# Two quads of matrices to a block in the product stage, with one pool of eight PSUM banks

## The chip, the cores and the metric

The kernel runs on one core of one Trainium2 chip. The metric is the device time of one execution in microseconds (us). Five engines each run their own instructions in order: TensorE (PE in the profile; its weight loads are listed as PEld), VectorE (DVE), ScalarE (ACT), GpSimd (POOL) and SyncE (SP), which here issues most transfers (DMAs). They wait for each other on semaphores. [...]

## The reference

The reference is a network of two layers on 16 images of 128 channels and 32 x 32 pixels. The first layer has an attention, then a part that convolves the 1024 tokens of an image with 16 long filters and mixes the channels with a matrix for each filter. The second layer has two 3 x 3 convolutions and a mixture of experts. The change lies in the long convolution, which the reference computes with Fourier transforms:

```python
Vf = jnp.fft.rfft(phi, n=n, axis=0)
Uf_p = jnp.fft.rfft(u, n=n, axis=1)
Uf_m = jnp.fft.rfft(u * sgn3, n=n, axis=1)
U_plus = jnp.fft.irfft(Vf[None, :, :, None] * Uf_p[:, :, None, :], n=n, axis=1)[:, :sl]
U_minus = jnp.fft.irfft(Vf[None, :, :, None] * Uf_m[:, :, None, :], n=n, axis=1)[:, :sl]
...
out = jnp.einsum('btkd,k,kde->bte', U_plus, s, Mpp)
out = out + jnp.einsum('btkd,k,kde->bte', U_minus, s, Mpm)
```

For one frequency the filters and the channel matrices fold into one complex matrix of 128 x 128, and what is left is its product with the 16 spectra of the images.

## The kernel before, in words

The kernel has three parts in time: the first layer up to the spectra, with the folding of the filters (0 to 395 us of the profiled execution), the product stage (395 to 684 us), and the inverse transform with the second layer (from 684 us).

The product stage handles the frequencies in 16 chunks (NCH). For each chunk c there are:

- The spectra v. `begin(c)` loads them from device memory (vd) in four transfers of four images each into `xc` (L764, SP), adds and subtracts their halves (L767, two instructions a transfer, POOL) and writes a negated copy (L768, one a transfer, POOL). v has two buffers, each xc one.
- The matrices g. `generate(c, q)`, for eight quads q, multiplies the folded filters `mst` with `ph` (L776, TensorE). Each product uses 32 rows of TensorE, so four of them (index r) stand beside each other, each with its own PSUM bank `pg`; a quad has 16 products. TensorE splits each float32 product into two, so the trace shows 32 records for a quad. Then the four banks are copied to SBUF: r = 1 by VectorE (L783), r = 3 by VectorE except in every fourth quad, the others by ScalarE (L785). g has two buffers, one for even chunks and one for odd.
- The product. `multiply(c, m, x, py, fresh)` multiplies g with v (L796, TensorE), for four values of m and two halves x. Each product uses 32 columns of TensorE; again 16 products, 32 records. Both halves of an m go to one bank `py`.
- The combination. The first half of py is copied to SBUF as `yt` (L822, ScalarE), and VectorE writes the sum and the difference of the second half, read from PSUM, and yt into `ys` (L824, L825). After the four m of a chunk four more additions follow (L832 to L835, POOL, in the last chunk VectorE), and ys is stored to device memory (yd) in two transfers (L839, SP). The next stage loads yd again (L945).

In the text, the loop (L808 to L842) puts one quad of chunk c+1 ahead of one half of chunk c, so that TensorE changes between them sixteen times a chunk, and `begin(c + 1)` comes first in a chunk. Six PSUM banks serve the quads (`psg`), two the sums (`psy`). In this stage the order of the instructions on each engine is left to the framework's scheduler, which starts from the text; in the two stages beside it, `tc.manual_schedule(engines=PINNED)` keeps the order of the text on PE, DVE, ACT and POOL. SP is not in PINNED. A tile of a pool waits until one of the pool's buffers is released by everything that read it.

Of the kernel before, what the change touches and what calls it, by code (L numbers as in the profile page):

```python
# [8 lines left out]
F32 = mybir.dt.float32  # L9
AF = mybir.ActivationFunctionType  # L10
ALU = mybir.AluOpType
AX = mybir.AxisListType
PSUM = bass.MemoryType.PSUM

P = 128
B, C, H, W = 16, 128, 32, 32
# [15 lines left out]
NM = NQ // 2  # L32
NCH = 16
JL = 8
CW = 2 * 2 * NM * JL
# [5 lines left out]
RG = P // KR  # L41
# [4 lines left out]
PINNED = {  # L46
    mybir.EngineType.PE, mybir.EngineType.DVE, mybir.EngineType.Activation, mybir.EngineType.Pool,
}
# [18 lines left out]
def metaformer_kernel(ctx: ExitStack, tc: tile.TileContext, io: dict, out: bass.AP):  # L67
    nc = tc.nc
# [26 lines left out]
    for n, (g_, b_, m_, v_) in enumerate(((V_G1, V_B1, V_M1, V_V1), (V_G2, V_B2, V_M2, V_V2))):  # L95
# [15 lines left out]
                name=nc.get_next_instruction_name(), ins=[], outs=[], act_func_set_id=EXP_LN  # L111
# [52 lines left out]
    with ExitStack() as l0:  # L164
# [581 lines left out]
        with ExitStack() as g0:  # L746
            gpl = [g0.enter_context(tc.tile_pool(name=f"gpl{i}", bufs=1)) for i in range(2)]
            cpl = g0.enter_context(tc.tile_pool(name="cpl", bufs=2))
            xcl = g0.enter_context(tc.tile_pool(name="xcl", bufs=1))
            psg = g0.enter_context(tc.tile_pool(name="psg", bufs=6, space=PSUM))  # L750
            psy = g0.enter_context(tc.tile_pool(name="psy", bufs=2, space=PSUM))
            gs, vs = {}, {}
            NB = EPR // 4

            def begin(c):

                gs[c] = gpl[c % 2].tile([P, CW, C], F32, name="g", tag="g")
                v = cpl.tile([P, 2 * NM * JL, 3, B], F32, name="v", tag="v")
                vs[c] = v
                vv = v.rearrange("p (x w) k b -> p x k b w", x=2)  # L760
                for i in range(B // BP):
                    bs = slice(i * BP, (i + 1) * BP)
                    xc = xcl.tile([P, BP, 2, 2, NM * JL], F32, name="xc", tag=f"xc{i}")
                    nc.sync.dma_start(xc.rearrange("p b x r w -> p b (x r w)"), vd[c, :, bs, :])  # L764
                    e, o = (xc[:, :, x].rearrange("p b r w -> p r b w") for x in range(2))
                    for x, op in enumerate((ALU.add, ALU.subtract)):
                        nc.gpsimd.tensor_tensor(vv[:, x, 1:, bs], e, o, op)  # L767
                    nc.gpsimd.tensor_scalar(v[:, :, 0, bs], v[:, :, 2, bs], -1.0, None, ALU.mult)  # L768

            def generate(c, q):  # L770

                pg = [psg.tile([P, 4, CW], F32, name="pg", tag="pg") for r in range(RG)]
                for i in range(4):
                    for r in range(RG):
                        rs = slice(r * KR, (r + 1) * KR)
                        nc.tensor.matmul(  # L776
                            pg[r][:, i], mst[rs, 4 * q + i, :], ph[rs, c, :], start=True, stop=True,
                        )
                for r in range(RG):
                    dst = gs[c].rearrange("p w (g q i) -> p g q w i", g=RG, q=NB)[:, r, q]  # L780
                    src = pg[r].rearrange("p i w -> p w i")
                    if r % 2 and (r == 1 or q % 4):
                        nc.vector.tensor_copy(dst, src)  # L783
                    else:
                        nc.scalar.copy(dst, src)  # L785

            def multiply(c, m, x, py, fresh):

                g, v = gs[c], vs[c]
                for kl in range(JL // RG):  # L790
                    for ri in range(2):
                        for grp in range(RG):
                            jl = RG * kl + grp
                            rows = slice(grp * 2 * B, (grp + 1) * 2 * B)

                            nc.tensor.matmul(  # L796
                                py[rows, x, kl, :],
                                v[:, (x * NM + m) * JL + jl, 1 - ri : 3 - ri, :]
                                .rearrange("p k b -> p (k b)"),
                                g[:, ((x * 2 + ri) * NM + m) * JL + jl, :],  # L800
                                start=(grp not in fresh), stop=(ri == 1), skip_group_check=True,
                            )
                            fresh.add(grp)

            begin(0)
            for q in range(NB):
                generate(0, q)
            for c in range(NCH):  # L808
                if c + 1 < NCH:
                    begin(c + 1)  # L810

                ys = cpl.tile([P, JL // RG, 2, NM, C], F32, name="ys", tag="ys")
                for m in range(NM):
                    py = psy.tile([P, 2, JL // RG, C], F32, name="py", tag="py")
                    fresh = set()
                    for x in range(2):
                        if c + 1 < NCH:
                            generate(c + 1, 2 * m + x)
                        multiply(c, m, x, py, fresh)
                        if x == 0:  # L820
                            t = cpl.tile([P, JL // RG, C], F32, name="yt", tag="yt")
                            nc.scalar.copy(t, py[:, 0])  # L822

                    nc.vector.tensor_tensor(ys[:, :, 0, m], py[:, 1], t, ALU.add)  # L824
                    nc.vector.scalar_tensor_tensor(  # L825
                        ys[:, :, 1, m], py[:, 1], -1.0, t, ALU.mult, ALU.add
                    )

                eng = nc.gpsimd if c + 1 < NCH else nc.vector
                e = cpl.tile([P, JL // RG, 2, C], F32, name="ye", tag="ye", bufs=1)  # L830
                yv = ys[:, :, 0]
                eng.tensor_tensor(e, yv[:, :, :2], yv[:, :, 2:], ALU.add)  # L832
                eng.tensor_tensor(yv[:, :, 2:], yv[:, :, :2], yv[:, :, 2:], ALU.subtract)
                eng.tensor_tensor(yv[:, :, 0], e[:, :, 0], e[:, :, 1], ALU.add)
                eng.tensor_tensor(yv[:, :, 1], e[:, :, 0], e[:, :, 1], ALU.subtract)  # L835
                for kl in range(JL // RG):
                    last = c + 2 >= NCH
                    j0 = kl * RG + (c - NCH + 2 if last else c) * JL
                    nc.sync.dma_start(  # L839
                        yd[last][j0 : j0 + RG].rearrange("g r b x e -> (g r b) (x e)"),  # L840
                        ys[:, kl].rearrange("p x m e -> p (x m e)"),
                    )  # L842


    gpool = ctx.enter_context(tc.tile_pool(name="gpool", bufs=1))
# [9 lines left out]
    with ExitStack() as c1:  # L855
# [557 lines left out]
        def collect(g, og):  # L1413

            pt = ps.tile([P, EG, CG], F32, name="pot", tag="s", bufs=1)
            nc.tensor.transpose(pt.rearrange("p i b -> p (i b)"), og, ident)
            nc.vector.tensor_copy(
                ot[:, :, g * EG : (g + 1) * EG].rearrange("p b i -> p i b"), pt[:, :, :B]
            )
# [34 lines left out]
        with tc.manual_schedule(engines=PINNED):  # L1454
            for pr in (7, *range(NPAIR - 1)):
                py = [ps.tile([P, N], F32, name=f"pfy{j}", tag="pfy") for j in range(2)]
# [7 lines left out]
                for j in range(2):  # L1464
                    b = 2 * pr + j
                    if j and pr % 2:
                        t = first.tile([P, N], F32, name="yt", tag="v", bufs=2)
# [133 lines left out]
```

## Time and profile before

| | |
|---|---|
| time, median of three runs | 1324.6 us (1319.44 to 1328.2) |
| span of the profiled execution, first to last instruction | 1322.2 us |
| product stage in it: first quad to last addition | 395.8 to 684.3 us |
| chunk in the middle of the stage | 16.91 us |
| TensorE busy in the span | 1216.7 us (92%) |
| L776, the quads | 155.3 us busy, 4096 records |
| L796, the products | 140.1 us busy, 4096 records |
| L785, copies of g by ScalarE | 153.1 us, 288 of 591 ns |
| L783, copies of g by VectorE | 145.8 us, 224 of 687 ns |
| L767, sums for v by POOL | 91.6 us, 128 of 741 ns |

The profiled execution's time is known as its span; what lies around the span is not listed. A line of the trace in order of time gives the start, the duration in us, the engine, the line of the kernel, the operation, the tile written and those read, the shapes and the number of instructions merged, and in brackets how long the engine was idle before and what ended that. "issue" means that it waited for nothing that the profile shows. Records of matmuls overlap, since a product starts while those before it are still on their way.

### The profile page before, as it was taken

How to read it: one execution, taken by the hardware profiler on the slowest of the kernel's cores; microseconds unless marked ns; L12 is line 12 of the kernel's file. 1: busy time of each engine (PE TensorE's matmuls, PEld its weight loads, DVE VectorE, ACT ScalarE, POOL GpSimd, SP SyncE). 2: the span in 40 equal slices, each digit the busy share in tenths (PEclk: the TensorE clock that was granted, in tenths of full speed). 3: DMA queues.
4: the chain of work that ended last, by engine and by line, in shares of the span. 5: the costliest groups of instructions: out<-in, count | busy, mean ns of one | idle time of the engine just before them, and what ended most of it. 6: DMA issues, size and time to landing. Idle time of an engine off the chain costs nothing. (4 is left out here: it accounts for less than half of the span.)

```text
span 1322.2 us, 33734 instructions
## 1 busy us (share of the span) xinstructions
PE 1216.7 (92%) x14116; PEld 990.8 (75%) x14116; DVE 907.2 (69%) x1982; ACT 705.2 (53%) x1424; POOL 503.3 (38%) x816
## 2 busy tenths in 40 slices
PE   4889999999998999999956999999999999996886
PEld 3777777777767888888846987989888888883443
DVE  5688887877765666776637767777778676772224
ACT  3777777777545666666623435545555454544111
POOL 2324545454685777777743111222212121110002
PEclk8899999999998999999987999999999999997998
DMA  7014343433344333333367211313122113007986
GB/s 268 17 35 140 118 134 112 144 124 121 114 149 145 127 125 127 127 121 119 107 235 182 70 48 49 88 27 111 32 80 64 33 49 127 17 24 260 374 329 255
DMA packets 87401, 162.99 MB, mean 123 GB/s; under 512 B 5584, under 2 KB 40784, under 8 KB 86864
## 3 DMA queue, kind: packets, MB, share of 16 engines
q1 hardware_dynamic: 86608, 158.33, 36.2%
q8 instruction: 111, 1.82, 0.6%
q0 software_dynamic: 640, 2.49, 0.5%
q14 instruction: 42, 0.34, 0.1%
HBM read 104.18 MB, written 56.62 MB: 122 GB/s over the span
## 5 line engine op out<-in xcount | busy, mean ns | idle before, releaser
L926 PE MATMUL pcv<-v,cw 128*128 128x256 f32 x1536 | 342.9, 380 | 0.0
L926 PEld LDWEIGHTS pcv<-v,cw 128*128 128x128 f32 x1536 | 286.8, 190 | 42.2 <-issue 5.7
L785 ACT COPY g<-pg 128x512 f32<-128x512 f32 x288 | 153.1, 591 | 102.8 <-PE pg L776 102.8
L783 DVE COPY g<-pg 128x512 f32<-128x512 f32 x224 | 145.8, 687 | 90.1 <-PE pg L776 90.1
L776 PE MATMUL pg<-ph,mst 32*128 32x128 f32 x4096 | 155.3, 287 | 4.5 <-ACT g L785 3.0
L776 PEld LDWEIGHTS pg<-ph,mst 32*128 32x128 f32 x4096 | 130.7, 190 | 30.8 <-issue 25.9
L796 PE MATMUL py<-g,v 128*32 128x128 f32 x4096 | 140.1, 276 | 3.8 <-POOL v L768 1.2
L796 PEld LDWEIGHTS py<-g,v 128*32 128x32 f32 x4096 | 105.3, 110 | 20.7 <-issue 2.4
L767 POOL TENSOR_TENSOR v<-xc 128x256 f32<-128x256 f32 x128 | 91.6, 741 | 71.6 <-PE py L796 62.5
L141 ACT ACTIVATE tok<-tok,sts 128x128 f32<-128x128 f32 x256 | 101.8, 481 | 23.8 <-POOL sts L1001 20.4
L132 DVE BATCH_NORM_STATS2 bst<-big 128x6 f32<-128x256 f32 x256 | 91.1, 417 | 19.5 <-PE big L154 12.1
L1066 POOL TENSOR_SCALAR sts<-bst 128x8 f32<-128x8 f32 x16 | 6.5, 406 | 235.7 <-DVE bst L132 235.7
L920 DVE TENSOR_TENSOR v<-pads 128x544 f32<-128x544 f32 x128 | 85.0, 723 | 9.9 <-ACT pads L1119 9.5
L618 PE MATMUL big<-u,mu 128*128 128x128 f32 (+4 forms) x384 | 86.0, 380 | 0.0
L274 POOL TENSOR_TENSOR xf<-ab 128x256 f32<-128x256 f32 x34 | 24.8, 730 | 132.0 <-DVE ab L241 131.9
L618 PEld LDWEIGHTS big<-u,mu 128*128 128x128 f32 x384 | 56.7, 191 | 18.0 <-issue 15.4
L1097 ACT ACTIVATE ct<-pcv,bn 128x256 f32<-128x256 f32 x64 | 30.3, 474 | 68.8 <-PE pcv L926 67.9
L551 PE MATMUL big<-wf,ub 128*128 128x256 f32 x256 | 62.0, 385 | 0.2
L149 PEld LDWEIGHTS big<-ident,x 128*128 128x128 f32 x384 | 47.3, 148 | 19.2 <-issue 7.2
L149 PE MATMUL big<-ident,x 128*128 128x128 f32 x384 | 53.6, 286 | 8.5 <-DVE x L1048 3.4
L1115 DVE TENSOR_TENSOR r<-pcv,cs 128x256 f32<-128x256 f32 x64 | 26.9, 420 | 49.0 <-PE pcv L926 48.2
L141 ACT ACTIVATE tt<-tt,sts 128x128 f32<-128x128 f32 x128 | 51.1, 480 | 9.2 <-POOL sts L1001 8.9
(231 smaller groups left out, 2271.3 us busy)
## 6 DMA issues: line engine op xcount, KB each, us to landing
we<-in_weight SPq DMA_DIRECT2D x32, 1024.0 KB, 9.7
vd<-xf SPq DMA_DIRECT2D x16, 1024.0 KB, 5.1
xc<-vd SPq DMA_DIRECT2D x64, 256.0 KB, 3.5
yd<-ys SPq DMA_DIRECT2D x32, 512.0 KB, 3.8
y<-yd SPq DMA_DIRECT2D x15, 896.0 KB, 6.5
x<-in_x SPq DMA_DIRECT2D x16, 512.0 KB, 4.1
mi<-in_M_phi SPq DMA_DIRECT2D x16, 512.0 KB, 4.9
xd<-x SPq DMA_DIRECT2D x16, 512.0 KB, 6.0
```

The costliest lines, as they stand in the source:

```text
L132: nc.vector.bn_stats(bst[:, j : j + 2, :].rearrange("p j s -> p (j s)"), src[:, j : j + 2, :].rearrange("p j c -> p c j"),)
L141: nc.scalar.activation(dst[:, j, :], src[:, j, :], AF.Identity, bias=nm[:, j : j + 1], scale=r[:, j : j + 1],)
L149: nc.tensor.transpose(pt[:, j, :], src[:, j * P : (j + 1) * P], ident)
L551: nc.tensor.matmul(dst, self.ub[:, q, :], wf[:, q, :], start=True, stop=True)
L618: nc.tensor.matmul(self.pa[:, a:hi], mu[:, NF - 1 - si, tap, :], self.u[:, a - tap : hi - tap], start=(tap == 0), stop=(tap == KU - 1),)
L767: nc.gpsimd.tensor_tensor(vv[:, x, 1:, bs], e, o, op)
L776: nc.tensor.matmul(pg[r][:, i], mst[rs, 4 * q + i, :], ph[rs, c, :], start=True, stop=True,)
L783: nc.vector.tensor_copy(dst, src)
L785: nc.scalar.copy(dst, src)
L796: nc.tensor.matmul(py[rows, x, kl, :], v[:, (x * NM + m) * JL + jl, 1 - ri : 3 - ri, :] .rearrange("p k b -> p (k b)"), g[:, ((x * 2 + ri) ...
L920: nc.vector.tensor_tensor(v[:, k], d[i], d[j], op)
L926: nc.tensor.matmul(pc[:, i], wt[:, dy, k, :], v[:, k, hf * HR + dy : hf * HR + dy + HR], start=(dy == 0), stop=(dy == 2),)
```

## The change

A block of the loop now has two quads of chunk c+1 and then both halves of one m of chunk c, so there are four blocks a chunk. `generate` is split: it only makes the products, and `collect` copies them out. A block's order in the text is: both quads, the copies of the first, the combination of the block before (`combine`, and after the last m of a chunk `finish`), then, in the first block of a chunk, `begin(c + 1)`, the copies of the second quad, both halves, and one ScalarE copy of all of py to `t`. The combination therefore reads both operands from t in SBUF. t has one buffer of twice the size. All PSUM tiles of the stage come from one pool of eight banks under one tag. The whole stage stands under `manual_schedule`. The number of products, of copies of g and of operations on POOL is as before.

```diff
-            psg = g0.enter_context(tc.tile_pool(name="psg", bufs=6, space=PSUM))
-            psy = g0.enter_context(tc.tile_pool(name="psy", bufs=2, space=PSUM))
+            psg = g0.enter_context(tc.tile_pool(name="psg", bufs=8, space=PSUM))
...
             def begin(c):
 
-                gs[c] = gpl[c % 2].tile([P, CW, C], F32, name="g", tag="g")
...
-                pg = [psg.tile([P, 4, CW], F32, name="pg", tag="pg") for r in range(RG)]
+                pg = [psg.tile([P, 4, CW], F32, name="pg", tag="p") for r in range(RG)]
...
+                return pg
+
+            def collect(c, q, pg):
+
                 for r in range(RG):
...
-            begin(0)
-            for q in range(NB):
-                generate(0, q)
-            for c in range(NCH):
-                if c + 1 < NCH:
-                    begin(c + 1)
-
-                ys = cpl.tile([P, JL // RG, 2, NM, C], F32, name="ys", tag="ys")
-                for m in range(NM):
-                    py = psy.tile([P, 2, JL // RG, C], F32, name="py", tag="py")
-                    fresh = set()
-                    for x in range(2):
-                        if c + 1 < NCH:
-                            generate(c + 1, 2 * m + x)
-                        multiply(c, m, x, py, fresh)
-                        if x == 0:
-                            t = cpl.tile([P, JL // RG, C], F32, name="yt", tag="yt")
-                            nc.scalar.copy(t, py[:, 0])
-
-                    nc.vector.tensor_tensor(ys[:, :, 0, m], py[:, 1], t, ALU.add)
-                    nc.vector.scalar_tensor_tensor(
-                        ys[:, :, 1, m], py[:, 1], -1.0, t, ALU.mult, ALU.add
-                    )
+            def finish(c, ys):
 
                 eng = nc.gpsimd if c + 1 < NCH else nc.vector
...
+            def combine(c, m, ys, t):
+
+                nc.vector.tensor_tensor(ys[:, :, 0, m], t[:, 1], t[:, 0], ALU.add)
+                nc.vector.scalar_tensor_tensor(
+                    ys[:, :, 1, m], t[:, 1], -1.0, t[:, 0], ALU.mult, ALU.add
+                )
+                if m == NM - 1:
+                    finish(c, ys)
+
+            with tc.manual_schedule(engines=PINNED):
+                begin(0)
+                gs[0] = gpl[0].tile([P, CW, C], F32, name="g", tag="g")
+                for q in range(NB):
+                    collect(0, q, generate(0, q))
+                waiting = None
+                for c in range(NCH):
+                    if c + 1 < NCH:
+                        gs[c + 1] = gpl[(c + 1) % 2].tile([P, CW, C], F32, name="g", tag="g")
+
+                    ys = cpl.tile([P, JL // RG, 2, NM, C], F32, name="ys", tag="ys")
+                    for m in range(NM):
+                        if c + 1 < NCH:
+                            pg = [generate(c + 1, 2 * m + x) for x in range(2)]
+                            collect(c + 1, 2 * m, pg[0])
+                        if waiting:
+                            combine(*waiting)
+                        if c + 1 < NCH:
+                            if m == 0:
+                                begin(c + 1)
+                            collect(c + 1, 2 * m + 1, pg[1])
+                        py = psg.tile([P, 2, JL // RG, C], F32, name="py", tag="p")
+                        fresh = set()
+                        for x in range(2):
+                            multiply(c, m, x, py, fresh)
+                        t = cpl.tile([P, 2, JL // RG, C], F32, name="yt", tag="yt", bufs=1)
+                        nc.scalar.copy(t, py)
+                        waiting = c, m, ys, t
+                combine(*waiting)
```

## The prediction

> **What bounds the kernel now.** I read the page's first part, then the windows of the product stage (395 to 684 us), then its order of time, and last the start of the next stage, which shows two engines that meet there as they will meet in the changed stage.
>
> ```profile
> PE 1216.7 (92%) x14116; PEld 990.8 (75%) x14116; DVE 907.2 (69%) x1982; ACT 705.2 (53%) x1424; POOL 503.3 (38%) x816
> 503.00:521.00 18.00, 18.00 (x555) 15.22 (x548) 12.55 (x24) 11.70 (x24) 13.82 (x18) 1.00 0.40 131
> ```
>
> In 18 us of the stage (columns PE, PEld, DVE, ACT, POOL, clock) TensorE is busy throughout at full clock, the others 65 to 77%. So the order on TensorE sets the time, and only what TensorE spends or waits counts.
>
> ```profile
> 504.18 0.98 PEld L776 LDWEIGHTS pg<-ph,mst 32*128 32x128 f32 x32 [0.20 <-issue]
> 504.50 0.41 DVE L824 TENSOR_TENSOR ys<-py,yt 128x256 f32<-128x256 f32 x1
> 504.83 0.41 DVE L825 SCALAR_TENSOR_TENSOR ys<-py,yt 128x256 f32<-128x256 f32 x1
> 505.28 0.81 PEld L796 LDWEIGHTS py<-g,v 128*32 128x32 f32 x32
> 505.37 1.07 ACT L785 COPY g<-pg 128x512 f32<-128x512 f32 x2 [1.04 <-PE pg L776]
> 505.41 1.29 DVE L783 COPY g<-pg 128x512 f32<-128x512 f32 x2 [0.17 <-PE pg L776]
> 506.29 0.98 PEld L776 LDWEIGHTS pg<-ph,mst 32*128 32x128 f32 x32 [0.20 <-issue]
> ...
> 674.52 1.77 PEld L796 LDWEIGHTS py<-g,v 128*32 128x32 f32 x64 [0.71 <-PE py L796]
> ```
>
> A quad is generated in 1.10 us (504.18 to 505.28), a half multiplied in 1.01: 2.11 together, 16.91 for a chunk of eight pairs. The 0.20 us ahead of each quad is put to "issue": TensorE waits for nobody, it changes from products 128x32 to 32x128. The single records show eight rounds of four in each train. Rounds follow at 0.112 (generate) and 0.109 us (multiply), but there is 0.218 to the first multiply round and 0.135 after it, 0.221 to the first generate round and 0.215 after it. Above the plain steps that is 0.107 + 0.026 + 0.111 + 0.103 = 0.347 us per pair of changes. The x64 row is two multiply trains without a gap; the stage's first load row, x36, runs from one quad into the next likewise.
>
> ```profile
> 694.94 0.43 DVE L965 TENSOR_TENSOR zt<-y 128x256 f32<-128x256 f32 x1 [10.63 <-DMA y<-yd]
> 694.96 0.99 POOL L958 TENSOR_TENSOR z<-y 128x256 f32<-128x256 f32 x1 [16.38 <-DMA y<-yd]
> 695.29 0.95 DVE L966 TENSOR_TENSOR zt<-y 128x256 f32<-128x256 f32 x1
> 695.91 0.90 POOL L959 TENSOR_TENSOR z<-y 128x256 f32<-128x256 f32 x1
> 696.16 0.94 DVE L967 TENSOR_TENSOR zt<-y 128x256 f32<-128x256 f32 x1
> 697.02 0.41 DVE L968 TENSOR_TENSOR zt<-y 128x256 f32<-128x256 f32 x1
> ```
>
> Here VectorE's operands both lie in SBUF while POOL reads SBUF. An operation of 0.41 us takes 0.95, POOL's of 0.73 takes 0.90 to 0.99, by turns. L824 and L825 above, with one operand in PSUM, take 0.41 although POOL is at work beside them.
>
> **The change, part by part.** T is the start of a block's first quad, T' of the next block's.
>
> *TensorE.* A block is now two quads and two halves with one pair of changes where there were two: 2 x 2.114 - 0.347 = 3.88 us. There are 15 chunks of 4 blocks with quads: 60 x 0.347 = 20.8 us less. The first block gains some 0.6 more: POOL's v still ends at 414.9, but both quads of that block then lie ahead of it, in time that TensorE now spends waiting (414.95 is the first multiply after a wait of 1.4).
>
> *The last chunk* has no quads. Now it takes from 670.2 to 682.2, because each half waits for a copy (L822) or an addition. Then it is 64 rounds x 0.109 = 7.0, the last product's end 0.27, copy 0.59, two additions 0.74, steps between 0.3: 8.9. I take 2.9 less; at worst nothing, since POOL's v for this chunk is due 2 us earlier than elsewhere. Gross gain 20.8 + 0.6 + 2.9 = 24.3.
>
> *Banks.* Eight banks hold both quads, and the sum py takes the first that is copied out: T + 1.19 + 0.59 = 1.8, needed at T + 2.0. The next block's first quad needs three others and one of the second quad, copied by about T + 3.3. Its second quad, due at T' + 1.0, needs all that are left: py and those of the second quad. py: its last product ends near T', the copy starts 0.18 after T' (as L822 does now) and is out at T' + 0.8, which fits by 0.2.
>
> *ACT.* The copy grows from 0.39 to 0.59 us and comes once a block where there were two: 5 x 0.59 + 0.59 = 3.5 at most of 3.88. It costs nothing while it ends before T' + 1.0. Its target t has one buffer where there were two, so it also waits for the additions on the t before: they end by T + 3.7 + r, in the worst case 0.3 after the copy could start, less than the stall on VectorE that r then makes anyway.
>
> *VectorE.* The two additions now stand between the copies of both quads; behind them wait the second quad's copies, and behind these the next second quad on TensorE. Additions alone: 0.33 + 0.33 us from start to start. In a block with odd m (two copies a quad, 0.60 apart): 1.24 + 2 x 0.60 + 0.67 + 0.60 + 0.69 = T + 4.40 = T' + 0.52; it fits. But the operand that was in PSUM is now t in SBUF, and POOL works through most of a chunk: 1.24 + 1.23 + 0.70 + 0.69 (L832 to L835) and 4 x (0.70 + 0.70 + 0.82) (L767, L768) = 12.7. From the rows at 694.94: the first addition waits for what is left (r) of POOL's operation, which keeps VectorE out for 0.60; then they alternate at 0.60 + 0.26 = 0.86. So the pair takes r + 0.86 + 0.33 in place of 0.67, and the last copy is out at T' + 1.04 + r: with 0.05 to TensorE a stall of 0.09 + r. r is between 0 and 0.60; I take the middle, 0.30, as nothing fixes the phase: 0.39 a stall. In even blocks ACT takes one of the copies, 0.60 less, and there is no stall; in the first block of a chunk POOL stands idle, since it waits for these very additions. So two stalls a chunk, 29 in all: 11.3 us back (2.6 to 20).
>
> [...]
>
> *POOL and SP.* The end of chunk c-1 (four operations, two yd stores) now stands ahead of the beginning of chunk c+1 (12 operations, four xc loads), and waits for the additions: from T0 + 2.6 (T0: start of the chunk), where POOL now starts v at T0 + 0.1. 2.6 + 12.7 + 1.6 held by VectorE (6 x 0.26) = T0 + 16.9; v is needed at T0 + 16.3 + 2.0. Covered by 1.4; if that cover goes, each us beyond costs 14 us. SP is not in the pinned set: xc is loaded as soon as POOL has freed its buffer, a chunk ahead, before the yd of the chunk after. I cost the move of six DMA issues at nothing for that reason. Moving the allocation of g issues nothing.
>
> **Sum.** 24.3 - 11.3 = 13.0. The profiled span of 1322.2 becomes 1309.2; the median shown, 1324.6, is 2.4 above that span (start and end outside it, and scatter), so 1311.6. With the bounds of r: 1303 to 1320.
>
> **Rivals.**
> 1. The additions don't meet POOL, or VectorE's slack takes it up. For: the overlaps of this kind are few and all in the next stage. Against: each of those with POOL's 256-element operations holds one engine or the other. Then 1324.6 - 24.3 = 1300.3.
> 2. Each engine keeps the other out for its whole instruction: the pair takes r + 0.41 + 0.73 + 0.33, 0.28 more, and r averages 0.37. A stall is then 0.74, 29 of them 21.5; 24.3 - 21.5 = 2.8 less: 1321.8. Against: L967 at 696.16 would then have ended 0.41 behind the end of L959, at 697.22; it ended at 697.10. [...]
> 3. The change loses: SP issues the xc loads behind the yd stores of the chunk before. Finish ends at T0 + 6.5, two stores 0.8, a load lands in 3.5 (the table of DMA issues), v 8.9 and 1.0 held: T0 + 20.7, needed at the chunk's length + 2.0: chunks of 18.7 against 16.91, +1.8 x 14 = 25, less 0.9 for the first block and 2.9: 1345.8. It decides once v comes after T0 + 18.9. For: that is the order in the text. Against: SP now waits 192.6 us in the stage for POOL's release of xc buffers (60 times), so the loads run ahead.
> 4. Another loss: the banks come back in another order, so that the first quad of a block waits for the last copy, due 1.0 sooner: 29 x (0.39 + 1.0) = 40 against 24.3: 1340.6. Nothing in the trace speaks for or against it: with six banks no choice was left.
> 5. It doesn't do what it says: the 0.20 stays at the boundary of two quads. The x36 row excludes it but for the first.
>
> **Chances.** My sum with its bounds 0.56, rival 1 0.19, rival 2 0.08, rival 3 0.10, rival 4 0.07. The measurement tells about 1% from no change, that is below 1311.4 and above 1337.8. My sum lies at the lower bound: half of it is faster. Faster 0.28 + 0.19 = 0.47; same 0.28 + 0.08 = 0.36; slower 0.17. The range leaves out the losses and reaches to rivals 1 and 2 with their scatter: 1298 to 1328; for the sum alone 1303 to 1320.
>
> **What would show it.** One gap of 0.20 a block ahead of L776, 60 and not 118; blocks of 3.88 us, some 0.4 longer where VectorE is late, with "ACT" or "DVE g" as releaser of L776 there. The additions at 0.41 in the first block of a chunk and up to 0.95 in the other three. POOL's wait ahead of L832, not of L767. If chunks take 15.5, the meeting is harmless; over 18, look at v on POOL and the xc issues on SP; if L776's first product waits, at the banks. I would be wrong above all through the phase r, which no row fixes.

## The result, and the profile after

| | before | after |
|---|---|---|
| median of 20 executions each | 1322.22 us (1317.93 to 1332.84) | 1316.17 us (1309.85 to 1326.12) |
| ratio after to before | | 0.9952, 95% interval 0.9935 to 0.997 |
| span of the profiled execution | 1322.2 us | 1322.4 us |
| first quad to first product of the next stage, in it | 298.97 us | 292.44 us |

The change gains 6.3 us by the ratio (0.0048 x 1322). 13.0 us were forecast. The gain is less than the 1% that the prediction takes as the bound of "no change", but the interval shows that it is above zero.

The two profiled spans are equal, so I first had to find where this execution of after lost its gain. The first product of the next stage comes at 694.73 us in before and at 687.65 in after, 7.1 earlier; the routing products `pp`, much later, end at 1216.27 and 1208.59, 7.7 earlier. From there to the end before takes 105.9 us and after 113.8. The windows view of the same 30 us in both (columns: stretch, length, PE, PEld, DVE, ACT, POOL, granted clock, DMA share, GB/s), before and then after:

```profile
1195.00:1225.00 30.00, 19.03 (x137) 9.57 (x141) 6.82 (x11) 9.43 (x15) 0.00 (x0) 0.77 0.67 241
```

```profile
1195.00:1225.00 30.00, 20.34 (x130) 9.17 (x130) 6.99 (x12) 5.33 (x7) 0.00 (x0) 0.54 0.53 180
```

The granted clock is the last column but two: 0.77 against 0.54. Behind the change's stage the granted clock of after was 0.50 from 1196.1 to 1223.4 us, that of before was 0.50 from 1196.5 to 1199.9 and from 1206.8 to 1217.0. A single execution can lie that far off without any change of the kernel: over the 20 executions of after the mean granted clock goes from 0.963 to 0.972, the time goes with it (correlation -0.85, 13.5 us for 0.01), and the profiled execution is one of those with the least, 0.964. Whether the change also lowers the clock in the mean is open: the means of the variants below lie from 0.004 above to 0.005 below that of before on the same chip. A comparison of two single executions of this kernel can therefore err by 12 us, twice the effect. Stages have to be compared one by one.

The stage itself, in the windows view of after, over the same 18 us as before:

```profile
503.00:521.00 18.00, 17.93 (x584) 16.26 (x577) 14.80 (x27) 12.65 (x25) 14.84 (x18) 1.00 0.42 141
```

TensorE is still listed as busy throughout, but with 584 records against 555: its trains are closer. VectorE goes from 70% to 82%, with three more instructions and with longer ones. A part of the chunk in order of time:

```profile
500.52 1.88 PEld L774 LDWEIGHTS pg<-ph,mst 32*128 32x128 f32 x64 [0.20 <-issue]
502.52 1.69 PEld L798 LDWEIGHTS py<-g,v 128*32 128x32 f32 x64
502.70 1.63 POOL L765 TENSOR_TENSOR v<-xc 128x256 f32<-128x256 f32 x2
502.96 0.77 DVE L826 TENSOR_TENSOR ys<-yt 128x256 f32<-128x256 f32 x1
503.65 0.96 DVE L827 SCALAR_TENSOR_TENSOR ys<-yt 128x256 f32<-128x256 f32 x1
504.41 1.19 PEld L774 LDWEIGHTS pg<-ph,mst 32*128 32x128 f32 x36 [0.20 <-issue]
...
505.86 0.97 PEld L774 LDWEIGHTS pg<-ph,mst 32*128 32x128 f32 x28 [0.26 <-DVE g L785]
506.95 1.69 PEld L798 LDWEIGHTS py<-g,v 128*32 128x32 f32 x64
508.83 1.88 PEld L774 LDWEIGHTS pg<-ph,mst 32*128 32x128 f32 x64 [0.20 <-DVE g L785]
...
514.56 0.41 DVE L826 TENSOR_TENSOR ys<-yt 128x256 f32<-128x256 f32 x1
515.06 1.39 POOL L812 TENSOR_TENSOR ye<-ys 128x512 f32<-128x512 f32 x1 [2.65 <-DVE ys L826]
```

The reader is to see four things. A block without a stall takes 3.89 us (500.52 to 504.41), one with a stall 4.42 (504.41 to 508.83). The switch shows as 0.20 once a block, whatever name stands behind it: "DVE g" with 0.20 is the same switch, with a copy that ended meanwhile. The additions take 0.77 and 0.96 us while POOL makes v, and 0.41 when POOL waits. And where they are late the stall stands inside the train, as x36 and x28 with 0.26 between, ahead of the rest of the second quad; the row shows half of what the block loses. Over chunks 1 to 14, the groups by form:

```profile
L765 POOL TENSOR_TENSOR v<-xc 128x256 f32<-128x256 f32 x112 | 88.2, 811 | 0.0
L766 POOL TENSOR_SCALAR v<-v 128x256 f32<-128x256 f32 x56 | 49.1, 876 | 4.9
L827 DVE SCALAR_TENSOR_TENSOR ys<-yt 128x256 f32<-128x256 f32 x56 | 43.3, 773 | 0.0
L826 DVE TENSOR_TENSOR ys<-yt 128x256 f32<-128x256 f32 x56 | 30.8, 550 | 0.0
```

The sums of 0.41 us have become 0.55 and 0.77 in the mean (0.966 at most), POOL's of 0.74 have become 0.81. The meeting that the prediction argued for is there.

From the single records, the stage splits like this (us, after minus before; the parts are rounded; "stalls" are counted in the two blocks of a chunk where they were forecast, and "other gaps" is all else that the trains lose):

| part | forecast | measured |
|---|---|---|
| first quad to chunk 1 (four pairs of switches gone: 1.4) | -2.0 | -1.5 |
| switches of chunks 1 to 14, 56 x 0.347 | -19.4 | -19.4 |
| stalls of quads behind VectorE, chunks 1 to 14 | +11.3 | +6.7 |
| other gaps in the trains | 0 | +6.3 (7.6, less 1.3 that before had) |
| last chunk and transfers up to the next stage's first product | -2.9 | +1.5 |
| sum | -13.0 | -6.5 |

What the "other gaps" are, the prediction did not know. One of them in order of time, and then the table of transfers for the microsecond before it:

```profile
459.02 2.64 SPq L762 DMA_DIRECT2D xc<-vd  x2
460.72 0.30 PE L798 MATMUL py<-g,v 128*32 128x128 f32 x1
461.17 0.42 DVE L826 TENSOR_TENSOR ys<-yt 128x256 f32<-128x256 f32 x1
462.08 1.95 PE L798 MATMUL py<-g,v 128*32 128x128 f32 x63 [1.06 <-issue]
```

```profile
DMA packets 64, 0.14 MB, mean 143 GB/s; under 512 B 1, under 2 KB 1, under 8 KB 63
q1 hardware_dynamic: 63, 0.13, 45.8%
q8 instruction: 1, 0.02, 5.9%
```

TensorE issues one product of sixty-four and then nothing for 1.3 us, with "issue" as releaser: no semaphore, no data, no bank. In the microsecond ahead of that one packet of 16 KB moves on queue q8, "instruction", among 63 packets of the xc loads; it ends at 460.57 and TensorE goes on 1.5 us later. Such a packet comes once in about 256 records of TensorE (q8 has 111 in the whole execution, before and after, for 28232 records of products and weight loads; in the stage one every 4.13 us in after, 4.26 in before). The idea at this point: TensorE is waiting for its own instructions, whose packets are held up by data. The experiments test it.

### The profile page after: what moved, and what is told of

Read it like the earlier page. It is cut to its first block, busy times and chain, and to the rows that moved or that the text cites. A ratio compares the mean times of both kernels' runs of the same rounds, so it can differ in the third digit from the quotient of the medians.

```text
span 1322.4 us, 33679 instructions
## 1 busy us (share of the span) xinstructions
PE 1209.1 (91%) x14116; PEld 996.3 (75%) x14116; DVE 932.7 (71%) x1982; ACT 715.7 (54%) x1424; POOL 517.0 (39%) x816
## 4 chain that ended last, share of the span: by engine, by line
PE 83%; DVE 6%; DMA 3%; ACT 3%; POOL 2%; issue 1%; SPq 0%; POOLq 0%; ACTq 0%; DVEq 0%
PE pcv L945 25%; PE pg L774 9%; PE py L798 8%; PE big L618 6%; PE big L149 4%; PE big L159 4%; PE big L1058 4%; PE big L551 3%; PE big L418 2%; PE pc L482 2%; PE big L514 2%; PE big L436 2%; DVE bst L132 2%; PE big L1206 1%; PE ph L1400 1%
## 5 line engine op out<-in xcount | busy, mean ns | idle before, releaser
L787 ACT COPY g<-pg 128x512 f32<-128x512 f32 x288 | 147.3, 604 | 32.2 <-PE pg L774 32.1
L774 PE MATMUL pg<-ph,mst 32*128 32x128 f32 x4096 | 143.8, 279 | 4.1 <-issue 2.3
L774 PEld LDWEIGHTS pg<-ph,mst 32*128 32x128 f32 x4096 | 129.1, 186 | 19.8 <-issue 8.9
L798 PE MATMUL py<-g,v 128*32 128x128 f32 x4096 | 127.6, 276 | 9.3 <-POOL v L765 5.6
L798 PEld LDWEIGHTS py<-g,v 128*32 128x32 f32 x4096 | 110.1, 111 | 18.1 <-POOL v L765 5.8
L132 DVE BATCH_NORM_STATS2 bst<-big 128x6 f32<-128x256 f32 x256 | 91.2, 418 | 19.1 <-PE big L154 12.1
L765 POOL TENSOR_TENSOR v<-xc 128x256 f32<-128x256 f32 x128 | 99.5, 801 | 9.3 <-DVE g L785 9.3
L859 ACT COPY yt<-py 128x512 f32<-128x512 f32 x64 | 37.5, 585 | 65.9 <-PE py L798 44.4
```

The source lines that it names most:

```text
L132: nc.vector.bn_stats(bst[:, j : j + 2, :].rearrange("p j s -> p (j s)"), src[:, j : j + 2, :].rearrange("p j c -> p c j"),)
L774: nc.tensor.matmul(pg[r][:, i], mst[rs, 4 * q + i, :], ph[rs, c, :], start=True, stop=True,)
L798: nc.tensor.matmul(py[rows, x, kl, :], v[:, (x * NM + m) * JL + jl, 1 - ri : 3 - ri, :] .rearrange("p k b -> p (k b)"), g[:, ((x * 2 + ri) ...
```

## The experiments

Each ratio is to the kernel before on the same chip; "stage" is first quad to first product of the next stage (before 298.97, after 292.44), read from the one profiled execution of each kernel, so its scatter isn't known. The theory to begin with was that of the prediction: the switches bring 0.347 us a block, and the meeting of VectorE and POOL in SBUF takes it back. Line numbers of the variants may differ by a few from those of after.

**Without the cause of the meeting.** From chunk 2 on there are no loads of xc and no sums on POOL.

```diff
                             if m == 0:
-                                begin(c + 1)
+                                if c == 0:
+                                    begin(1)
+                                else:
+                                    vs[c + 1] = vs[c - 1]
```

> This kernel leaves out part of the computation: v is loaded and summed only for chunks 0 and 1, later chunks multiply with these again, so POOL has only its four closing operations a chunk and SP no xc loads. Theory (the additions, now with both operands in SBUF, meet POOL, so the second quad's copies and then TensorE are late): from chunk 2 on the additions of m = 1 and 2 take 0.41 us and the second quads go on without a gap: the 6.7 us of gaps inside the trains of quads in the blocks m = 2 and m = 0 fall below 1, chunks go from 16.6 to 15.6 us, and the last chunk's wait for v (1.45 us) goes: 8 to 9 us less than the changed kernel, 14 to 15 less than the one before (ratio 0.989). Rival (the second quad waits for ScalarE's late copy of py, not for VectorE): the gaps stay at 6 to 7 us, and the time falls by the 1.45 alone. Second question: the gaps with the releaser issue (about 7 us, not expected). If the xc loads are behind them, they go too; if TensorE's own faster pace is, they stay.

Measured: ratio 0.9828 (0.98 to 0.9855), stage 279.75, chunks of 15.52. The loads of weights in order of time, chunk after chunk:

```profile
502.00 1.88 PEld L774 LDWEIGHTS pg<-ph,mst 32*128 32x128 f32 x64 [0.20 <-DVE g L785]
503.99 1.69 PEld L798 LDWEIGHTS py<-g,v 128*32 128x32 f32 x64
505.88 1.88 PEld L774 LDWEIGHTS pg<-ph,mst 32*128 32x128 f32 x64 [0.20 <-DVE g L785]
507.88 1.69 PEld L798 LDWEIGHTS py<-g,v 128*32 128x32 f32 x64
509.76 1.88 PEld L774 LDWEIGHTS pg<-ph,mst 32*128 32x128 f32 x64 [0.20 <-DVE g L785]
```

Blocks of exactly 3.88, and 4 x 3.88 = 15.52: the price of a switch was right, the banks and the copies keep up, and all that is given back comes from begin. But it gave more than the stalls behind VectorE: the gaps put to "issue" are gone too (0.05 us left ahead of the products). What in begin makes them, the loads or the sums?

**The loads without the sums.** The same, but the xc loads stay; POOL reads only eight numbers of each tile, so that its buffers come free.

```diff
+                                    vs[c + 1] = vs[c - 1]
+                                    touch(c + 1)
...
+            def touch(c):
+                for i in range(B // BP):
...
+                    nc.sync.dma_start(xc.rearrange("p b x r w -> p b (x r w)"), vd[c, :, bs, :])
+                    d = cpl.tile([P, 8], F32, name="xd", tag="xd", bufs=1)
+                    nc.gpsimd.tensor_scalar(d, xc[:, 0, 0, 0, 0:8], -1.0, None, ALU.mult)
```

> As the run without v, this leaves out v's sums from chunk 2 on, but keeps the xc loads: POOL reads eight numbers of each loaded tile. It separates the two things that went there: VectorE's meetings with POOL and the gaps with the releaser issue. Theory (the gaps are TensorE's waits for its own instructions, whose packets are held up by the xc loads): the gaps in the quads behind late copies stay away, but gaps of 0.3 to 1.5 us in front of the first multiplication or at the end of a quad train return, 2 to 6 us in the stage, each ending 1.2 to 1.6 us after the end of an instruction packet: 1306 to 1310, chunks 15.6 to 15.9 us. Rival (the gaps come from POOL's semaphores for v or from VectorE's lateness): no such gaps, chunks 15.52 as without loads.

Measured: ratio 0.9994 (0.9966 to 1.0022), stage 290.38. The quads stall for 0.04 us in the whole stage, so POOL's sums are the cause of all stalls behind VectorE. But TensorE now waits 12.2 us ahead of or within its products. One of the gaps in order of time, with the loads ahead of it, and the transfers of the microsecond from 538 to 539:

```profile
532.97 2.67 SPq L773 DMA_DIRECT2D xc<-vd  x4
536.81 1.88 PEld L783 LDWEIGHTS pg<-ph,mst 32*128 32x128 f32 x64 [0.20 <-DVE g L794]
538.81 0.14 PEld L807 LDWEIGHTS py<-g,v 128*32 128x32 f32 x2
540.40 1.68 PEld L807 LDWEIGHTS py<-g,v 128*32 128x32 f32 x62 [1.45 <-issue]
```

```profile
DMA packets 175, 0.33 MB, mean 330 GB/s; under 512 B 21, under 2 KB 21, under 8 KB 174
q1 hardware_dynamic: 174, 0.31, 84.2%
q8 instruction: 1, 0.02, 5.5%
```

The instruction packets of this stretch lie at 524.43, 528.20, 531.53 and then 538.07 us: 3.3 to 3.8 apart, and then 6.5, while four xc loads, issued together, move at 330 GB/s. This one ends at 538.95; TensorE goes on at 540.40, 1.45 later. The eleven gaps of over 0.45 us between two weight loads from 432 to 660 us all end 1.1 to 1.6 us after a packet's end, and they come about once a chunk, as the loads do. With the loads gone (above) there is one gap of that size, with them eleven: the loads hold up TensorE's instructions. The kernel before, whose trains use up 256 records in 4.2 us where the changed one needs 3.88, has one such gap, of 0.6.

The gaps also stand where a packet ends. In every kernel here, chunks 1 to 14 have 56 packets, one for the 256 records (128 loads and 128 products) of a block, so the edge between two packets stays at nearly the same record from block to block. In this run every gap comes behind two loads of the products (x2 and x62 above). In after the gaps come there or a load earlier in chunks 1 to 4, and from chunk 5 on 64 to 58 loads into the quads (the longest, 1.48 us, until 643.47).

In the whole time little of this shows: 0.9994 is level with before, where 1306 to 1310 us were expected. The ten executions took 1314.67 to 1331.28 us, and the profiled one is the fastest of them, so a stage of 290.38 may be less than usual.

**Fewer copies on VectorE.** ScalarE makes the r = 3 copy of the first quad in every block, so VectorE has time for the longer additions.

```diff
-                    if r % 2 and (r == 1 or q % 4):
+                    if r % 2 and (r == 1 or q % 2):
```

> One condition is changed: ScalarE makes three of the four copies of the first quad in every block, not in every second one, so VectorE has three copies a block. Theory: the additions meet POOL as before (0.41 to 0.97 us), but VectorE has 0.6 us more in blocks of odd m, so the second quad's last copy is out in time and the gaps inside the trains of quads fall from 6.7 us to below 1.5: 5 to 6 us less than the changed kernel, ratio to the kernel before 0.991. Rival (ScalarE's copy of py is what the second quad waits for): ScalarE has a copy more ahead of it, so the gaps grow and the time with them, by 0.5 us a block of odd m, some 14 us more, ratio above 1.

Measured: ratio 0.9919 (0.9895 to 0.9942), stage 288.84. In the two blocks of a chunk that the prediction named, stalls fall from 6.7 to 1.2 us. The "issue" gaps stay at 5.6. So the two costs are separate, and the first was VectorE's lateness. The stage got 3.6 us shorter and not 5.5, among other things because two products now wait 1.03 and 0.79 us (until 510.19 and 526.77), by the trace for ScalarE's copies. But both waits stand where a packet of instructions ends and end 1.46 and 1.44 us after it, so they may be of the other kind.

**begin ahead of the combination.** In the text begin(c + 1) comes before the additions, as before the change.

```diff
+                        if c + 1 < NCH and m == 0:
+                            begin(c + 1)
                         if waiting:
                             combine(*waiting)
                         if c + 1 < NCH:
-                            if m == 0:
-                                begin(c + 1)
```

> POOL's beginning of the next chunk stands ahead of the additions and the end of the chunk before. Theory: v starts some 2.6 us earlier in a chunk, so the wait of the last chunk for v (1.45 us) goes. The additions of m = 3 of the chunk before now meet POOL too, but in a block where VectorE has a copy less; those of m = 3 come when POOL has finished, so the gaps behind them (blocks m = 0) go, those behind m = 1 stay: 3 to 5 us less than the changed kernel, ratio 0.992. Rival (the stores of yd are late then and cost more): the closing operations end 9 us later in a chunk, and if the two-buffered ys is short, chunks grow beyond 16.6 us.

Measured: ratio 1.002 (0.9995 to 1.0044), stage 302.90. A miss. Stalls of the quads, here in all four blocks of a chunk, are 9.5 us (8.3 in after), gaps with "issue" as releaser 12.1 (6.2; the 7.6 of the table above has the other parts of the trains with it). The order of the change is the better one, by 10.5 us of the stage; 5.9 of that are more "issue" gaps and 1.2 more stalls, the rest I have not traced.

**Six banks and two.** The new order with the old split of the banks.

```diff
-            psg = g0.enter_context(tc.tile_pool(name="psg", bufs=8, space=PSUM))
+            psg = g0.enter_context(tc.tile_pool(name="psg", bufs=6, space=PSUM))
+            psy = g0.enter_context(tc.tile_pool(name="psy", bufs=2, space=PSUM))
...
-                        py = psg.tile([P, 2, JL // RG, C], F32, name="py", tag="p")
+                        py = psy.tile([P, 2, JL // RG, C], F32, name="py", tag="py")
```

> The order of the change with the banks of the kernel before: six for the quads, two for the sums. Theory (the order needs eight banks in common): the third and fourth bank of the second quad come from the first quad's copies, T + 1.97 where the quad is due at T + 1.0, so 0.97 us a block: 60 x 0.97 = 58 less the 6.7 us of gaps that VectorE then has time for: some 50 us above the changed kernel, ratio to the kernel before 1.033. Rival (the gain of the longer blocks doesn't hang on the banks): within 1% of the changed kernel.

Measured: ratio 1.0287 (1.0253 to 1.032), stage 339.39. The weight loads in order of time:

```profile
502.73 1.19 PEld L775 LDWEIGHTS pg<-ph,mst 32*128 32x128 f32 x36 [0.20 <-issue]
504.55 1.11 PEld L775 LDWEIGHTS pg<-ph,mst 32*128 32x128 f32 x28 [0.64 <-ACT g L788]
505.79 1.69 PEld L799 LDWEIGHTS py<-g,v 128*32 128x32 f32 x64
```

Every block stalls ahead of its second quad (x36, x28) for want of two banks, about 1.06 us each: chunks take 19.78 where 15.52 is the time without a stall. The pool of eight is a condition for the order. It is also a control for the other finding: at this slower pace the instruction packets come every 4.95 us, and the "issue" gaps are gone (0.04).

**The end of the stage, first try.** The four last additions of chunk 14 go to VectorE, as those of chunk 15 do, so that POOL doesn't stand in the way of the last additions.

```diff
-                eng = nc.gpsimd if c + 1 < NCH else nc.vector
+                eng = nc.gpsimd if c + 2 < NCH else nc.vector
```

> The four closing operations of chunk 14 move from POOL to VectorE, as those of chunk 15 are there already. Theory for the last chunk (VectorE's additions meet POOL's closing operations of chunk 14, which start only behind the clearing of pads, and one t buffer makes each copy wait for them): no addition of the last chunk is stretched, and from the last quad's end to the last addition it takes 12.5 us and not 14.8: 2 us less than the changed kernel, ratio to the kernel before 0.994. Rival (the last chunk is long because of its wait for v alone): at most 0.5 us change, or 2 us more, since VectorE has 2.2 us more to do.

Measured: ratio 0.9951 (0.993 to 0.9971), stage 292.57. The last additions end some 2.1 us earlier after the quads, and the next stage starts no earlier: something else ends the stage. With ScalarE's copies in addition:

> The two edits together: ScalarE makes three copies of every first quad, and the closing operations of chunk 14 are on VectorE. If both theories hold and add, the ratio to the kernel before is 0.990, 2 us better than the copies alone; if VectorE's additional 2.2 us are on the last chunk's path, it is no better than 0.992.

Measured: ratio 0.9951 (0.9929 to 0.9973), stage 291.09. It doesn't add to the 0.9919 either.

**The order left to the framework's scheduler**, as it was before the change: only `manual_schedule` is taken away.

> The change without the pinned order: the framework's scheduler places the product stage's instructions, as before the change. Theory (the gain comes from the order on TensorE and costs VectorE's lateness): if the scheduler keeps two quads and two halves together, it may place the additions behind the second quad's copies where they hold up nothing, and the time is that of the changed kernel or up to 6 us less. Rival (the pinned order is what keeps the pairs together): TensorE changes more often, and the time goes back to that of the kernel before, ratio 1.00.

Measured: ratio 0.9999 (0.9978 to 1.0021), stage 296.84, "issue" gaps 12.8 us, stalls 4.1. Without the fixed order most of the gain is lost. The time is that of the rival, but not by its mechanism: in chunks 1 to 14 there are still two quads and two halves in turn (64 loads of weights each). Against after, the "issue" gaps are 6.6 us more and the stalls 4.2 less; the other 2.0 of the 4.4 us of the stage I have not traced, nor why the gaps are more.

**The end of the stage, second try.** The transfers of the convolution weights cw go behind the first two images' loads of the next stage.

```diff
-        for n in range(2):
-            nc.sync.dma_start(cw[n], cwd[n])
...
             for b in range(2):
                 load(b)
+            for n in range(2):
+                nc.sync.dma_start(cw[n], cwd[n])
```

> The changed kernel with one thing more: the two transfers of the convolution weights cw (L913) are issued behind the first two images' loads of the next stage, no longer ahead of the last yd stores and y loads. Same work, same bytes. Theory: the end of the product stage is set by the transfers that stand one behind the other (wi, cw, x, yd, y: 20.3 us from the issue of wi to the y load before, 20.5 after), so the last chunk's shorter work on TensorE bought nothing; with cw out of that line the first product of the next stage comes 3 to 4 us earlier than in the changed kernel, first quad to that product 289 instead of 292.4, and the ratio to the kernel before is about 0.9925. Rival: the y load waits only for the last yd store, and that for the last additions; then nothing moves, 292.4 and 0.995. It would also stay if cw is then missed by its first use, which would show as a wait on cw.

Measured: ratio 0.9934 (0.9902 to 0.9966), stage 287.36, 5.1 less than after. First the transfers' issues in after, with the first product of the next stage, then in this kernel, where the wait of the third image's transposes is shown too:

```profile
663.55 0.51 SPq L909 DMA_DIRECT2D wi<-wid  x1
664.11 0.90 SPq L913 DMA_DIRECT2D cw<-cwd  x2
670.68 6.55 SPq L819 DMA_DIRECT2D yd<-ys  x4
684.08 0.64 SPq L964 DMA_DIRECT2D y<-yd  x1
687.69 1.19 PE L1058 MATMUL big<-wi,y 128*128 128x128 f32 x4 [17.34 <-DMA y<-yd]
```

```profile
659.93 0.51 SPq L909 DMA_DIRECT2D wi<-wid  x1
667.23 6.53 SPq L819 DMA_DIRECT2D yd<-ys  x4
677.10 0.64 SPq L962 DMA_DIRECT2D y<-yd  x1
679.70 1.07 SPq L1362 DMA_DIRECT2D cw<-cwd  x2
704.03 1.94 PE L149 MATMUL big<-ident,x 128*128 128x128 f32 x8 [7.17 <-issue]
```

From wi to the first y load on SP there are 20.5 us in after and 17.2 here: the line of transfers paces the end, not the last additions. From the end of the last quad to the first product of the next stage it takes 24.3 us in place of 27.9, so 3.6 of the 5.1 come from the end; the other 1.5 lie ahead of it, where nothing was changed. But cw now stands ahead of the third image, and TensorE stands for 7.17 us ahead of its transposes (the trace names no releaser); from first product to first convolution product it takes 31.7 where after takes 28.1, so the 3.6 us are given back. With ScalarE's copies:

> The last change together with the copies of the second experiment (ScalarE makes the r = 3 copy of the first quad in every block, so that VectorE has one copy less ahead of the additions). Theory: the one shortens the chunks (288.84 from first quad to the first product of the next stage, ratio 0.992), the other the end of the stage (3 to 4 us), and they touch different places, so they add: about 285.5 and a ratio of about 0.989. Rival: the transfers at the end pace the stage whatever is moved, and the second experiment's 0.992 stays.

Measured: ratio 0.9922 (0.9892 to 0.9952), stage 288.57: the end is 3.7 us shorter than with the copies alone, but the chunks came out 3.4 longer, with more "issue" gaps (8.5 in place of 5.6).

**The third try** puts cw behind the third image's loads.

```diff
                 if self.b + 2 < B:
                     load(self.b + 2)
+                if self.b == 0:
+                    for n in range(2):
+                        nc.sync.dma_start(cw[n], cwd[n])
```

> The changed kernel with the two cw transfers issued still later, behind the loads of the third image, not behind those of the second. In the kernel with cw behind the first two images the first product of the next stage came 5.1 us earlier after the first quad than in the changed kernel, but TensorE then stood 7.2 us ahead of the third image's transposes (L149), and 3.6 us of the gain were gone by the first convolution product. Theory: the transfers run without a pause from wi on, so cw delays whatever is issued behind it; there it was the third image. Behind the third image it delays only what is needed after the first convolution products: the wait of 7.2 us falls to under 3, first quad to first product stays near 287.4, and the time from there to the first convolution product is near 28.1 again (31.7 with cw earlier). Ratio about 0.990. Rival: cw now lands after its first use, and the wait only moves from L149 to L943's first product: again 31 or more, and 0.993.

> The same move of cw together with ScalarE's r = 3 copy in every block. Theory: both gains, shorter chunks (3.6 us less in the second experiment) and the earlier end without the later wait: ratio about 0.988, and first quad to first product at 285 to 288. Rival: gaps of TensorE that wait for its own instructions fall differently in every kernel (5.6 to 8.5 us in the stage so far) and hide the sum: 0.991 to 0.992, as with either alone.

Measured: stage 288.43 and 286.79; to the first convolution product then 28.65 and 28.05. The wait ahead of the third image's transposes falls from 7.17 us to 1.4 and 2.7, as expected; in the first of the two kernels 3.7 us stand ahead of the second image's (1.3 in after). The place of the wait was understood: first quad to first convolution product is 328.0 in before, 320.5 in after, 317.1 and 314.8 here. In the whole time it can't be seen: ratios 0.9971 (0.9942 to 0.9999) and 0.9946 (0.9922 to 0.9969), where 0.990 and 0.988 were expected. The mean granted clock of these executions is 0.966 and 0.967, that of before beside them 0.971; at 13.5 us for 0.01 this would account for 6 to 7 us, but I have no run that holds the clock. The intervals of 0.9919, 0.9922, 0.9934 and 0.9946 overlap: that some version beats the changed kernel is seen in the stage of one profiled execution each, and for the whole time it is shown only that all lie below before.

## Why the prediction was right and wrong

The direction and the mechanism were right, and the time lies in the range; the gain is half of what was forecast. That it lies in the range is luck in part: the range of 1298 to 1328 us was made wide for the phase r and the rivals 1 and 2, and the losses that took half of the gain, gaps of instructions and a longer end, stand in none of them.

- *Switches*, 0.347 us a pair: right to the last digit. Blocks of 3.88 us, 60 switches and not 118, chunks of exactly 15.52 when nothing else is in the way. Worked out from the spacing of rounds in the records of before.
- *The first block*, 0.6: only about 0.1 came. The first product still waits for v.
- *Stalls behind VectorE*, 11.3 us with r = 0.30: 6.7, in the two blocks a chunk that were named. 29 stalls of 0.23 in place of 0.39 mean r = 0.14: the mechanism was right and the term was mis-sized, within its bounds (2.6 to 20). The run without sums (0.04 us of stalls) and the one with a copy less on VectorE (1.2) carry it. Additions of up to 0.966 us and 0.41 in a chunk's first block were forecast.
- *Rival 1*, no meeting: false for the kernel as it is. Its 1300.3 us is about what the kernel without begin took (1303.53, beside 1327.37 for before on that chip).
- *Rival 2*, each keeps the other out for its whole instruction, 0.74 a stall: not seen. An addition of 0.41 that lets one of POOL's of 0.73 go first would then take 1.14; the longest of the 112 in chunks 1 to 14 took 0.966. The row at the start of the next stage bounded it rightly there. In the last chunk the bound doesn't hold: an addition took 1.35 us beside two of POOL's operations of 256 elements (669.22 and 669.92), so the two don't always go by turns, and one took 1.97 beside an operation of 512 elements (667.27, 1.30 us) and a transfer that POOL issues (666.64); which of them held it was not tested.
- *Rivals 3 and 4*: the xc loads run ahead, and in chunks 1 to 14 no product waits for v; POOL's wait moved ahead of L812, 38.5 us in 14 waits, as forecast. No first product of a block waits for a bank, which needs the pool of eight.
- *The last chunk*, 2.9 less: failed, it took 1.5 more. (The prediction's own figures, 12.0 and 8.9, give 3.1; and rival 3 counts the first block with 0.9 where the sum has 0.6. Neither matters.) It was read as a chain of products, copies and additions. The row of VectorE and POOL at the start of the next stage, which the prediction quotes, has "DMA y<-yd" as its releaser with 10.63 and 16.38 us of waiting; the line of transfers that makes this wait starts when the last quad's products are done (SP waits for L774 until then) and doesn't get shorter with the additions. Moving cw out of it made the end 3.6 us shorter, ending the additions earlier brought none. POOL's finish of chunk 14 also stretched the last additions (1.09, 1.97 and 1.35 us at 665.88, 666.89 and 669.59), and v for this chunk came 1.45 late, both without effect behind that line.
- *What was missing*: 7.6 us of TensorE waiting for its instructions. "Only what TensorE spends or waits counts" was right, but the waits were looked for at semaphores alone. The sum had no term for them. Before has the queue "instruction" in its table of transfers, a packet for about 256 records, and one gap of 0.6.

The errors were of both signs: 4.6 us too much for stalls; 6.3 (7.6 less before's 1.3), 4.4 for the end of the stage and 0.5 for the first block too little.

Open: why the packets' gaps differ from kernel to kernel by some us (5.6 to 12.8 with the same loads). Where a packet ends in a block goes by the count of records (56 packets for the 56 blocks of chunks 1 to 14), but nothing here sets which packet meets the loads. Open too is whether loads in smaller pieces or spread over the chunk would spare the gaps; that wasn't tried.

## What to carry to other kernels

When one engine is busy all the time, price its change from one kind of product to another from the spacing of single records: that number, 0.347 us here, held exactly (blocks of 3.88). Then ask what the closer trains need that nothing showed before: another engine's slack, the buffers, and the engine's own instructions, whose packets are moved beside the data (in the microsecond shown 5.5% of the 16 DMA engines' time, the loads 84.2%). And before a shorter chain at the end of a stage is counted as gain, look at which wait ends last there; here it was a transfer in a line that had started 20.5 us earlier.

## What the runs showed of the hardware that was not expected

- The queue "instruction" (q8) moved 111 packets of 16 KB in an execution of after, 0.88 to 1.93 us long, one for about 254 of TensorE's 28232 records, so that the gaps of different blocks stood at nearly the same record. In the run with loads and no sums, while the loads moved at 330 GB/s, a packet came 6.5 us after the last in place of 3.3 to 3.8, and TensorE, which uses up 256 records in 3.88 us, went on 1.1 to 1.6 us after the packet's end. The longest such gap in after is 1.66 us from one weight load to the next (until 643.47). The profile puts these gaps to "issue", in the middle of a train. In the run with six banks and two, at 4.95 us for a packet, they came to 0.04 us.
- Changing between products that use 32 rows and products that use 32 columns cost 0.347 us for there and back in the records of before, and the run without begin, with one such pair a block, has blocks of 3.88 (2 x 2.114 - 0.347); the profile shows 0.20 of it as idle time of the weight loads.
- VectorE's addition of 128 x 256 numbers with both operands in SBUF took 0.41 us alone; in chunks 1 to 14, mostly beside POOL's operations of 256 elements, the two took 0.55 and 0.77 in the mean and 0.966 at most. In the last chunk one took 1.97.
- The granted clock of one core differed from execution to execution of the same kernel (0.963 to 0.972 in the mean over 20 executions of after), and the time went with it, by 12 us (13.5 us for 0.01).
